# Start of a convolution, window-attention and linear-attention kernel: half of the first band's depthwise convolution on TensorE, and the order of the first loads

## The chip, the cores and the metric

One core of a Trainium2 chip runs the kernel. The metric is the time of one execution on the device in microseconds (us). Before the change it is 968.08 us, the median of three runs (965.33 to 969.31). The profiled execution has a span of 963.5 us.

## The reference, cut to what matters

The input x has 4 images of 128 channels and 64 x 64 pixels. Only the first part of layer 0 is touched by the change: a normalization over the channels, a depthwise 3x3 convolution with edge padding that is added to its input, and the products with the attention weights in windows of 16 x 16 pixels. What follows is named so that the reader can place it.

```python
def _layernorm2d(x, g, b):
    mean = x.mean(axis=1, keepdims=True)
    var = ((x - mean) ** 2).mean(axis=1, keepdims=True)
    return (x - mean) / jnp.sqrt(var + EPS) * g + b

def _cpe(x, w, b):                      # depthwise 3x3, one 3x3 filter for each channel
    xp = jnp.pad(x, ((0, 0), (0, 0), (r, r), (r, r)), mode='edge')
    y = jax.lax.conv_general_dilated(xp, w, (1, 1), 'VALID', feature_group_count=x.shape[1], ...)
    return y + b[None, :, None, None]

y = _layernorm2d(x, ln_g, ln_b)
y = y + _cpe(y, cpe_w, cpe_b)
xw = ...                                # y cut into windows of 16 x 16
q, k, v = ...                           # xw times Wq, Wk, Wv: 2 branches of 4 heads of 32
# attention of each pixel to its 5 x 5 neighbours in its window, weights Wo, added to x
# layer 1: LayerNorm, causal linear attention (W, b), added; LayerNorm, product W,
#          normalization over all tokens, a recurrence over the 4096 tokens (V), added
```

## The kernel before

An image is taken in 4 bands of 16 rows, so there are 16 bands; a band has 4 windows. Channels lie on the 128 partitions after the turning. TensorE does the products, VectorE the statistics and the taps of the convolution, ScalarE the evictions from PSUM and the exponentials, GpSimd small things and the division of the attention's output. Each compute engine executes its instructions in the order in which the program writes them (`in_order`). A generator that yields marks a gap, a place where the loop puts other work.

Normalization of a band: statistics of groups of rows, scaling one step later, turning and eviction one more step later.

```python
def norm_rows(n):
    ...
    for g in range(len(groups) + 2):
        if g < len(groups):
            found[g] = measured([...], 1e-6)              # VectorE, and rs on GpSimd
        if g - 1 in found:
            xn[g - 1] = normed(found.pop(g - 1), p2, "xf")    # VectorE, waits for rs
        if g - 2 in xn:
            rows = turned(xn.pop(g - 2), 0, j1 - j0)...       # TensorE, by ident
            evict(y[...], rows[...])                          # ScalarE, into ypad
        yield
    # GpSimd copies the edges of ypad
```

The convolution as nine taps: the first on ScalarE, eight on VectorE. In the first band each window has its own taps (256 columns), in the others half a band (512 columns).

```python
def taps(y2, y, c0, width, each):
    for tap in range(9):
        dy, dx = divmod(tap, 3)
        src = y[:, dy : dy + WS, c0 + dx : c0 + dx + width]
        if tap == 0:
            nc.scalar.activation(y2, src, AF.Identity, bias=cpe_b, scale=cpe_w[:, 0:1])
        else:
            nc.vector.scalar_tensor_tensor(y2, src, cpe_w[:, tap : tap + 1], y2, ALU.mult, ALU.add)
        if tap % each == 0:
            yield

def convolve_first(wj):
    ...
    run(taps(y2, ypads.pop(0) if wj == NB - 1 else ypads[0], wj * WS, WS, 8))
```

A window: `window_inputs` makes q, k and v (products, ScalarE evictions, two small transfers that put together the middle block of v), `logits` the scores and their exponentials `es`, `weighted` the sums of the weights and the weighted values, `scaled` the division.

```python
def weighted(w):
    # TensorE: dps <- ones, es
    den = p1.tile(...)
    nc.scalar.copy(den, dps)
    nc.sync.dma_start(dc, den[::HD, :])
    yield
    # TensorE: ops <- es, v
    o_sb = p1.tile(...)                     # p1: one buffer
    nc.scalar.copy(o_sb, ops)
    yield
    nc.vector.tensor_tensor(dc, dc, pad_c, ALU.add)
    nc.vector.reciprocal(rc, dc)
    ...
    nc.sync.dma_start(rd.rearrange("h (a e) -> (h a) e", e=16), rc)           # to DRAM
    nc.sync.dma_start(rden, rd.unsqueeze(1).to_broadcast([HEADS, HD, BR * WT]))   # and back, spread
    ...
def scaled(n, wj, w):
    nc.gpsimd.tensor_tensor(oTs[n][...], w["o"]..., w["rden"]..., ALU.mult)   # oT <- o_sb, rden
```

The start and the loop over the windows. `front` brings the norm and convolution of the bands ahead, `layer1` the rest of the band behind, a step in each gap.

```python
load(0)
load_head(1)
load(1)
run(norm_rows(0))
convolve_first(0)
windows = {0: {}}
run(window_inputs(windows[0], 0, 0))
ahead, behind = front(), iter(())

def between(i, gap):
    next(behind, None)
    if i < len(places) and (i % NB or gap in (0, 4, 5)) and (i or gap):
        next(ahead, None)

for i in range(len(places) + 2):
    ...
    logits(windows[i])
    ...
    between(i, 0)
    ...                                     # scaled of window i - 2
    sums = weighted(windows[i - 1]) if 1 <= i <= len(places) else iter(())
    for gap in (1, 2):
        next(sums, None)
        between(i, gap)
    run(sums)
    if i == 0:
        convolve_first(1)
    ...                                     # inputs = window_inputs of window i + 1
    for gap in (3, 4, 5):
        next(inputs, None)
        between(i, gap)
    run(inputs)
    if i == 0:
        convolve_first(2)
        convolve_first(3)
```

Ahead of this, eighteen loads of weights are issued from ScalarE's queue, and woT, ab and the middle tap's weight are prepared on VectorE.

Of the kernel before, what the change touches and what calls it, by code (L numbers as in the profile page):

```python
# [9 lines left out]
F32 = mybir.dt.float32  # L10
BF16 = mybir.dt.bfloat16
AF = mybir.ActivationFunctionType
ALU = mybir.AluOpType
AX = mybir.AxisListType
PSUM = bass.MemoryType.PSUM
ENGINES = [getattr(mybir.EngineType, e) for e in ("PE", "DVE", "Activation", "Pool")]

P = 128
B, H, W = 4, 64, 64
T = H * W  # L20
WS = 16
NB = H // WS
WT = WS * WS
BR, HEADS, HD = 2, 4, 32
# [3 lines left out]
NCH = BAND // P  # L28
BIG = 1.0e30
LAM = 0.5  # L30
# [16 lines left out]
def conv_attn_hybrid(ctx: ExitStack, tc: tile.TileContext, ins: dict, out: bass.AP):  # L47
    nc = tc.nc

    fast = ExitStack()  # L50
    const = fast.enter_context(tc.tile_pool(name="const", bufs=1))
# [6 lines left out]
    def loaded(name, shape, dt=F32, src=None, eng=None):  # L58
        t = const.tile(shape, dt, name=name)
        (eng or nc.sync).dma_start(t, ins[name] if src is None else src)  # L60
        return t

    ident = const.tile([P, P], F32, name="ident")
# [17 lines left out]
    mhalf = const.tile([P, NCH], F32, name="mhalf")  # L81
    nc.vector.memset(mhalf, -0.5)

    ln_g = loaded("ln_g", [P, 1], eng=nc.scalar)
    ln_b = loaded("ln_b", [P, 1], eng=nc.scalar)
    cpe_w = loaded("cpe_w", [P, 9], eng=nc.scalar)
    cpe_b = loaded("cpe_b", [P, 1], eng=nc.scalar)
# [3 lines left out]
    mask_k = loaded("mask_k", [P, P], BF16, eng=nc.scalar)  # L91
    mask_q = loaded("mask_q", [P, BR * WT], BF16, eng=nc.scalar)
    pad_c = loaded("pad_c", [P, 16], eng=nc.scalar)
    woT = loaded("woT", [P, BR, P], eng=nc.scalar)
    awT = loaded("awT", [P, 3 * P], eng=nc.scalar)
    ab = loaded("ab", [P, 3], eng=nc.scalar)
    abv = loaded("abv", [P, P], src=ins["abv"].partition_broadcast(P), eng=nc.scalar)
    fwT = loaded("fwT", [P, P], eng=nc.scalar)
    fvT = loaded("fvT", [P, P], eng=nc.scalar)
    gamma = loaded("gamma", [P, 1], eng=nc.scalar)  # L100
    beta = loaded("beta", [P, 1], eng=nc.scalar)


    nc.vector.tensor_scalar(cpe_w[:, 4:5], cpe_w[:, 4:5], 1.0, None, ALU.add)

    rect = math.sqrt(1.0 + LAM * LAM * (BR - 1))
    nc.vector.tensor_scalar(woT[:, 0], woT[:, 0], 1.0 / rect, None, ALU.mult)
    nc.vector.tensor_scalar(woT[:, 1], woT[:, 1], LAM / rect, None, ALU.mult)

    ab1 = const.tile([P, 2], F32, name="ab1")  # L110
    nc.vector.tensor_scalar(ab1, ab[:, :2], 1.0, None, ALU.add)

    dmax = const.tile([P, 16], F32, name="dmax")
    nc.vector.memset(dmax, 1.0)
# [5 lines left out]
    for i in range(2):  # L120
        t = const.tile([P, 4, P + 1], F32, name=f"v1_{i}")
# [3 lines left out]
    stats = const.tile([P, B * T // 512, 6], F32, name="stats")  # L125

    wx = const.tile([P, B, NH, SEG, HSEGS], F32, name="wx")

    main = ExitStack()
    p1 = main.enter_context(tc.tile_pool(name="p1", bufs=1))  # L130
    p2 = main.enter_context(tc.tile_pool(name="p2", bufs=2))
    p3 = main.enter_context(tc.tile_pool(name="p3", bufs=3))
    px = main.enter_context(tc.tile_pool(name="px", bufs=3))
    p6 = main.enter_context(tc.tile_pool(name="p6", bufs=6))
    ps = main.enter_context(tc.tile_pool(name="ps", bufs=8, space=PSUM))

    first = len(nc.cur_bb.bb.instructions)

# [16 lines left out]
    def bank():  # L155
        return ps.tile([P, 512], F32, tag="bank", name="bank")

    def run(g):
        for _ in g:
            pass  # L160

    bands = [(b, wi) for b in range(B) for wi in range(NB)]
    scale = HD ** -0.5

    def measured(pieces, eps):
# [27 lines left out]
        return tps  # L193


    xin = {}
    ypads = {}
    y2s = {}

    heads = {}  # L200

    def load_head(n):
        b, wi = bands[n]
        heads[n] = p1.tile([P, P], F32, tag="head", name="head")
        nc.sync.dma_start(heads[n], ins["xt"][b, wi, :, 0, :])

    def load(n):
        b, wi = bands[n]
        xin[n] = p3.tile([P, NCH, P], F32, tag="xin", name="xin")
        nc.sync.dma_start(xin[n], ins["xt"][b, wi])  # L210

    def padded(n):
        if n not in ypads:
# [3 lines left out]
    def norm_rows(n):  # L217

        b, wi = bands[n]
        y = padded(n)  # L220
        below = wi < NB - 1
        first, end = (0 if wi == 0 else 1), NCH + below

        def evict(dst, src):
            nc.scalar.activation(dst, src, AF.Identity, bias=ln_b, scale=ln_g)

        groups = [(0, 4), (4, 8), (8, 9)] if wi == 0 else [(1, 5), (5, end)]

        found, xn = {}, {}
        for g in range(len(groups) + 2):  # L230
            if g < len(groups):
                found[g] = measured(
                    [xin[n][:, j, :] if j < NCH else heads.pop(n + 1) for j in range(*groups[g])],
                    1e-6,
                )
            if g - 1 in found:
                xn[g - 1] = normed(found.pop(g - 1), p2, "xf")
            if g - 2 in xn:
                j0, j1 = groups[g - 2]
                rows = turned(xn.pop(g - 2), 0, j1 - j0)[:, : (j1 - j0) * P]  # L240
                rows = rows.rearrange("p (r w) -> p r w", w=W)
                k1 = min(2 * j1 + 1, WS + 2)
                evict(y[:, 2 * j0 + 1 : k1, 1 : W + 1], rows[:, : k1 - 2 * j0 - 1, :])
                if j1 > NCH:
                    evict(padded(n + 1)[:, 1:3, 1 : W + 1], rows[:, 2 * (NCH - j0) :, :])
            yield
        ks = slice(1, WS + 1 + below)
        nc.gpsimd.tensor_copy(y[:, ks, 0:1], y[:, ks, 1:2])
        nc.gpsimd.tensor_copy(y[:, ks, W + 1 :], y[:, ks, W : W + 1])

        if wi == 0:
            nc.gpsimd.tensor_copy(y[:, 0, :], y[:, 1, :])
        if below:
            nc.gpsimd.tensor_copy(padded(n + 1)[:, 0, :], y[:, WS, :])
        else:
            nc.gpsimd.tensor_copy(y[:, WS + 1, :], y[:, WS, :])
# [10 lines that stand above are left out]
            if tap % each == 0:  # L267
                yield

    def convolve_first(wj):  # L270

        half, k = divmod(wj, 2)
        if k == 0:
            y2s[0, half] = p2.tile([P, 2, WT], F32, tag="y2w", name="y2w")
        y2 = y2s[0, half][:, k, :].rearrange("p (r c) -> p r c", c=WS)
        run(taps(y2, ypads.pop(0) if wj == NB - 1 else ypads[0], wj * WS, WS, 8))

    def convolve(n, half):

# [341 lines left out]
    def front():  # L621


        for n in range(1, len(bands)):
            yield from norm_rows(n)
            if bands[n][1]:
                yield
            for half in range(2):
                yield from convolve(n, half)
                yield  # L630

    load(0)
    load_head(1)
    load(1)
    run(norm_rows(0))
    convolve_first(0)
    windows = {0: {}}
    run(window_inputs(windows[0], 0, 0))
    ahead, behind = front(), iter(())

    def between(i, gap):


        next(behind, None)
        if i < len(places) and (i % NB or gap in (0, 4, 5)) and (i or gap):
            next(ahead, None)

    for i in range(len(places) + 2):
        if i < len(places):
            n, wj = places[i]  # L650
            if wj == 0 and n + 1 < len(bands) and bands[n + 1][1] < NB - 1:
                load_head(n + 2)
            logits(windows[i])
        if 2 <= i:
            m, wjm = places[i - 2]
            if wjm == NB - 1:
                run(behind)
                behind = layer1(m, halves.pop(m - 1, (None, None)))
        between(i, 0)
        if 2 <= i:  # L660
            scaled(m, wjm, windows.pop(i - 2))
        if i < len(places) and wj == 1 and n + 2 < len(bands):
            load(n + 2)
# [3 lines that stand above are left out]
            between(i, gap)  # L667
        run(sums)
        if i == 0:
            convolve_first(1)  # L670
        inputs = iter(())
        if i + 1 < len(places):
            windows[i + 1] = {}
            inputs = window_inputs(windows[i + 1], *places[i + 1])
        for gap in (3, 4, 5):
            next(inputs, None)
            between(i, gap)
        run(inputs)
        if i == 0:
            convolve_first(2)  # L680
            convolve_first(3)
    run(behind)
    run(layer1_end(*halves.pop(len(bands) - 1)))
    in_order()
# [78 lines left out]
    for s in range(SEG):  # L763
        ys = ring.tile([P, B * SEGS], F32, tag="ys", name="ys")
        for g in range(NG):
            z = seeded(g, s)
            nc.tensor.matmul(z, fvT, last[g], start=False, stop=True, skip_group_check=True)
            y = ys[:, g * GC : (g + 1) * GC]
# [698 lines left out]
```

## Time and profile before

| | before |
|---|---|
| median of 3 runs | 968.08 us |
| span of the profiled execution | 963.5 us |
| TensorE busy | 872.7 us (91%) |
| VectorE busy | 756.2 us (78%) |
| ScalarE busy | 541.2 us (56%) |
| GpSimd busy | 259.7 us (27%) |

In the profile, PE is TensorE's products, PEld its loading of weights, DVE VectorE, ACT ScalarE, POOL GpSimd, SP SyncE; SPq and ACTq are the queues from which transfers are issued. An entry names the line of the kernel, the engine, the operation, and what it writes and reads. The chain of waits goes back from the last instruction, at each step to what released it; "issue" is time in which nothing shown was waited for. The time from 94 us to 889 us belongs to the dense middle of the kernel, the rest to the end with the recurrence.

### The profile page before, as it was taken

How to read it: one execution, taken by the hardware profiler on the slowest of the kernel's cores; microseconds unless marked ns; L12 is line 12 of the kernel's file. 1: busy time of each engine (PE TensorE's matmuls, PEld its weight loads, DVE VectorE, ACT ScalarE, POOL GpSimd, SP SyncE). 2: the span in 40 equal slices, each digit the busy share in tenths (PEclk: the TensorE clock that was granted, in tenths of full speed). 3: DMA queues.
4: the chain of work that ended last, by engine and by line, in shares of the span. 5: the costliest groups of instructions: out<-in, count | busy, mean ns of one | idle time of the engine just before them, and what ended most of it. 6: DMA issues, size and time to landing. Idle time of an engine off the chain costs nothing.

```text
span 963.5 us, 26493 instructions
## 1 busy us (share of the span) xinstructions
PE 872.7 (91%) x10472; PEld 649.9 (67%) x10472; DVE 756.2 (78%) x2468; ACT 541.2 (56%) x1001; POOL 259.7 (27%) x359
## 2 busy tenths in 40 slices
PE   2587999999999999999999999999999999978884
PEld 1365777778676777767777777676776778655442
DVE  4554897988787878888787978897988887577796
ACT  1454666565666656565656565666656565622553
POOL 2112222322314131323232221414131312131175
PEclk9788999999999999999999999999999999999798
DMA  3011112111212121121212111212112111110853
GB/s 117 12 38 39 57 58 57 53 54 56 57 49 69 36 78 37 47 57 59 57 55 57 53 52 54 64 47 70 37 54 58 45 36 58 42 39 22 352 205 146
DMA packets 52902, 63.47 MB, mean 66 GB/s; under 512 B 22944, under 2 KB 33824, under 8 KB 52256
## 3 DMA queue, kind: packets, MB, share of 16 engines
q1 hardware_dynamic: 49888, 56.38, 18.7%
q10 hardware_dynamic: 2880, 5.29, 1.4%
q8 instruction: 85, 1.39, 0.6%
q14 instruction: 49, 0.40, 0.1%
HBM read 35.44 MB, written 17.30 MB: 55 GB/s over the span
## 4 chain that ended last, share of the span: by engine, by line
PE 71%; DVE 11%; DMA 9%; ACT 4%; POOL 2%; issue 2%; SPq 1%; ACTq 0%; POOLq 0%; DVEq 0%
PE bank L297 10%; PE bank L342 6%; PE bank L425 6%; PE bank L192 6%; PE bank L372 6%; PE bank L360 5%; PE bank L310 5%; PE bank L454 5%; DMA rden<-rd 5%; PE bank L533 3%; PE bank L497 3%; PE bank L562 3%; PE bank L514 3%; PE bank L535 3%; DMA res<-resd 2%; PE bank L471 2%
## 5 line engine op out<-in xcount | busy, mean ns | idle before, releaser
L266 DVE SCALAR_TENSOR_TENSOR y<-ypad,cpe_w,y 128x512 f32<-128x512 f32 x240 | 189.8, 791 | 11.1 <-ACT y L264 7.6
L400 POOL TENSOR_TENSOR oT<-o_sb,rden 128x512 f32<-128x512 f32 x64 | 83.0, 1297 | 357.6 <-DMA rden<-rd 308.0
L351 ACT ACTIVATE es<-bank 128x512 f32<-128x512 f32 x256 | 132.2, 602 | 75.5 <-PE bank L342 75.5
L176 POOL TENSOR_TENSOR rs<-rs,mhalf 128x4 f32<-128x4 f32 (+2 forms) x100 | 107.2, 1072 | 8.3
L342 PEld LDWEIGHTS bank<-q,k 32*128 32x128 f32 x3072 | 97.8, 189 | 7.5 <-ACT k L305 6.2
L342 PE MATMUL bank<-q,k 32*128 32x96 f32 (+1 forms) x3072 | 96.3, 270 | 5.6 <-ACT k L305 5.6
L183 DVE TENSOR_SCALAR xn<-x,mv,rs 128x128 f32<-128x128 f32 x256 | 83.5, 387 | 21.6 <-POOL rs L176 21.6
L175 POOL TENSOR_SCALAR rs<-mv 128x4 f32<-128x4 f32 (+2 forms) x100 | 25.1, 251 | 278.0 <-DVE mv L173 190.0
L297 PE MATMUL bank<-y2w,wqT 128*128 128x256 f32 x256 | 68.7, 392 | 13.9 <-DVE y2w L266 13.2
L372 PEld LDWEIGHTS bank<-es,v_sb 128*32 128x32 f32 x3072 | 57.4, 111 | 29.9 <-issue 17.1
L380 ACT COPY o_sb<-bank 128x512 f32<-128x512 f32 x64 | 37.6, 587 | 60.5 <-POOL oT L400 47.5
L372 PE MATMUL bank<-es,v_sb 128*32 128x96 f32 (+1 forms) x3072 | 70.9, 241 | 0.0
L425 PE MATMUL bank<-woT,oT 128*128 128x128 f32 x512 | 65.3, 282 | 5.8 <-POOL oT L400 5.8
L454 PE MATMUL bank<-xl,awT 128*128 128x512 f32 x128 | 70.1, 631 | 0.3 <-ACT xl L449 0.3
L360 PE MATMUL bank<-es,ones 128*32 128x512 f32 x512 | 69.9, 619 | 0.0
L425 PEld LDWEIGHTS bank<-woT,oT 128*128 128x128 f32 x512 | 62.1, 195 | 9.6 <-POOL oT L400 6.8
L317 ACT COPY v_sb<-bank 128x512 f32<-128x512 f32 x64 | 37.6, 588 | 54.2 <-PE bank L310 53.5
L297 PE MATMUL bank<-y2w,wkT 128*128 128x256 f32 x256 | 67.6, 388 | 0.0
L310 PE MATMUL bank<-wvT,y2w 128*128 128x256 f32 x256 | 67.6, 387 | 0.0
L297 PEld LDWEIGHTS bank<-y2w,wqT 128*128 128x128 f32 x256 | 46.1, 196 | 25.9 <-issue 14.5
L305 ACT COPY q<-bank 128x512 f32<-128x512 f32 x64 | 37.8, 590 | 45.8 <-PE bank L297 45.5
L192 PE MATMUL bank<-ident,xf 128*128 128x128 f32 x128 | 31.2, 331 | 35.0 <-DVE xf L183 30.8
(120 smaller groups left out, 1747.3 us busy)
## 6 DMA issues: line engine op xcount, KB each, us to landing
rden<-rd SPq DMA_DIRECT2D x64, 256.0 KB
xin<-in_xt SPq DMA_DIRECT2D x16, 512.0 KB
v_sb<-v_sb SPq DMA_DIRECT2D x128, 64.0 KB
resd<-rs_o SPq DMA_DIRECT2D x32, 256.0 KB
out<-ot SPq DMA_DIRECT2D x32, 256.0 KB
res<-resd SPq DMA_DIRECT2D x2, 2048.0 KB
res<-resd ACTq DMA_DIRECT2D x2, 2048.0 KB
dc<-den SPq DMA_DIRECT2D x64, 8.0 KB
```

The source lines that it names most:

```text
L176: nc.gpsimd.tensor_tensor(rs[:, :n], rs[:, :n], mhalf[:, :n], ALU.pow)
L183: nc.vector.tensor_scalar(xn[:, j, :], piece, mv[:, j, 0:1], rs[:, j : j + 1], ALU.subtract, ALU.mult)
L192: nc.tensor.transpose(tps[:, j * P : (j + 1) * P], xn[:, j0 + j, :], ident)
L266: nc.vector.scalar_tensor_tensor(y2, src, cpe_w[:, tap : tap + 1], y2, ALU.mult, ALU.add)
L297: nc.tensor.matmul(pps[:, br * WT : (br + 1) * WT], wT[:, br * P : (br + 1) * P], y2, start=True, stop=True,)
L310: nc.tensor.matmul(vps[:, e * 256 : (e + 1) * 256], y2[:, e * P : (e + 1) * P], wvT, start=True, stop=True,)
L342: nc.tensor.matmul(sps[h][:, cols], w["k"][rows, k0 : k0 + P], w["q"][rows, cols], start=False, stop=(br, n) == pieces[-1],)
L351: nc.scalar.activation(es, sps[h], AF.Exp, scale=scale)
L360: nc.tensor.matmul(dps[rows], ones[:, :HD], w["es", h], start=True, stop=True)
L372: nc.tensor.matmul(ops[rows, cols], w["v"][:, n, c0 : c0 + HD], w["es", h][:, cols], start=(br, n) == pieces[0], stop=(br, n) == pieces[-1],)
L425: nc.tensor.matmul(yps[:, j * P : (j + 1) * P], oT[:, br, t], woT[:, br, :], start=br == 0, stop=br == BR - 1,)
L454: nc.tensor.matmul(zps, awT[:, m * P : (m + 1) * P], h.xl, start=True, stop=True)
```

## The change

Half of the first band's convolution, windows 2 and 3, is done on TensorE: a depthwise convolution is nine products with diagonal weights, added up in PSUM. The nine diagonals are written by ScalarE from the identity, into a part of wx that is not yet in use. The taps of windows 0 and 1 stay on VectorE and are both put ahead of window 0's products; window 2's nine products are put around those of window 0, window 3's after the logits of window 0. This is to keep TensorE from standing while VectorE convolves. The loads of x come first, the first band's in two pieces; weights that are needed later are loaded from SyncE's queue behind x, and prepared after the taps, so that the first scaling of x doesn't stand behind them. The next band's norm begins one gap earlier, and four empty steps after the second band put the rest of the sequence where it was.

```diff
+    load(0, 2)
+    load_head(1)
     ln_g = loaded("ln_g", [P, 1], eng=nc.scalar)
     ...                                            # cpe_w, cpe_b, wqT, wkT, wvT, masks: as before
     pad_c = loaded("pad_c", [P, 16], eng=nc.scalar)
-    woT = loaded("woT", [P, BR, P], eng=nc.scalar)
-    awT = loaded("awT", [P, 3 * P], eng=nc.scalar)
-    ...                                            # ab, abv, fwT, fvT, gamma, beta
-    nc.vector.tensor_scalar(cpe_w[:, 4:5], cpe_w[:, 4:5], 1.0, None, ALU.add)
-    ...                                            # woT and ab prepared
+    load(1)
+    woT = loaded("woT", [P, BR, P])
+    awT = loaded("awT", [P, 3 * P])
+    ...                                            # ab, abv, fwT, fvT, gamma, beta
+    def prepare():
+        ...                                        # woT and ab prepared

+    diag = wx[:, B - 1].rearrange("p n s k -> p (n s k)")[:, : 9 * P]
+    diag = diag.rearrange("p (t c) -> p t c", c=P)
+
+    def multiply_first(wj):
+        half, k = divmod(wj, 2)
+        if k == 0:
+            y2s[0, half] = p2.tile([P, 2, WT], F32, tag="y2w", name="y2w")
+        y = ypads.pop(0) if wj == NB - 1 else ypads[0]
+        cps = bank()[:, :WT]
+        for tap in range(9):
+            dy, dx = divmod(tap, 3)
+            src = y[:, dy : dy + WS, wj * WS + dx : wj * WS + dx + WS]
+            nc.tensor.matmul(cps, diag[:, tap, :], src, start=tap == 0, stop=tap == 8)
+            if tap == 3:
+                yield
+        nc.scalar.activation(y2s[0, half][:, k, :], cps, AF.Identity, bias=cpe_b)

     # front()
+            if n == 1:
+                for _ in range(4):
+                    yield

-    load(0)
-    load_head(1)
-    load(1)
+    nc.vector.tensor_scalar(cpe_w[:, 4:5], cpe_w[:, 4:5], 1.0, None, ALU.add)
+    for tap in range(9):
+        nc.scalar.activation(diag[:, tap, :], ident, AF.Copy, scale=cpe_w[:, tap : tap + 1])
     run(norm_rows(0))
+    load_head(2)
     convolve_first(0)
+    convolve_first(1)
+    prepare()
+    third, fourth = multiply_first(2), multiply_first(3)
+    next(third)
     windows = {0: {}}
     run(window_inputs(windows[0], 0, 0))
+    run(third)

     # between(i, gap)
-        if i < len(places) and (i % NB or gap in (0, 4, 5)) and (i or gap):
+        if i < len(places) and (i == 0 or i % NB or gap in (0, 4, 5)):

     # the loop over the windows
-        if i == 0:
-            convolve_first(1)
+        if i == 0:
+            run(fourth)
     ...
-        if i == 0:
-            convolve_first(2)
-            convolve_first(3)
```

More of the change, by code (lines that the diff above doesn't have):

```diff
@@ L82, in conv_attn_hybrid, with load_head, load @@
     nc.vector.memset(mhalf, -0.5)
+    main = ExitStack()
+    p1 = main.enter_context(tc.tile_pool(name="p1", bufs=1))
+    p2 = main.enter_context(tc.tile_pool(name="p2", bufs=2))
+    p3 = main.enter_context(tc.tile_pool(name="p3", bufs=3))
+    px = main.enter_context(tc.tile_pool(name="px", bufs=3))
+    p6 = main.enter_context(tc.tile_pool(name="p6", bufs=6))
+    ps = main.enter_context(tc.tile_pool(name="ps", bufs=8, space=PSUM))
+    bands = [(b, wi) for b in range(B) for wi in range(NB)]
+    xin = {}
+    heads = {}
+    def load_head(n):
+        b, wi = bands[n]
+        heads[n] = p1.tile([P, P], F32, tag="head", name="head")
+        nc.sync.dma_start(heads[n], ins["xt"][b, wi, :, 0, :])
+    def load(n, pieces=1):
+        b, wi = bands[n]
+        xin[n] = p3.tile([P, NCH, P], F32, tag="xin", name="xin")
+        for k in range(pieces):
+            js = slice(k * NCH // pieces, (k + 1) * NCH // pieces)
+            nc.sync.dma_start(xin[n][:, js, :], ins["xt"][b, wi, :, js, :])
+    load(0, 2)
+    load_head(1)
     ln_g = loaded("ln_g", [P, 1], eng=nc.scalar)
@@ L93, in conv_attn_hybrid @@
     pad_c = loaded("pad_c", [P, 16], eng=nc.scalar)
-    woT = loaded("woT", [P, BR, P], eng=nc.scalar)
-    awT = loaded("awT", [P, 3 * P], eng=nc.scalar)
[L96 to L101, printed above, removed]
-    nc.vector.tensor_scalar(cpe_w[:, 4:5], cpe_w[:, 4:5], 1.0, None, ALU.add)
-    rect = math.sqrt(1.0 + LAM * LAM * (BR - 1))
-    nc.vector.tensor_scalar(woT[:, 0], woT[:, 0], 1.0 / rect, None, ALU.mult)
-    nc.vector.tensor_scalar(woT[:, 1], woT[:, 1], LAM / rect, None, ALU.mult)
-    ab1 = const.tile([P, 2], F32, name="ab1")
-    nc.vector.tensor_scalar(ab1, ab[:, :2], 1.0, None, ALU.add)
+    load(1)
+    woT = loaded("woT", [P, BR, P])
+    awT = loaded("awT", [P, 3 * P])
+    ab = loaded("ab", [P, 3])
+    abv = loaded("abv", [P, P], src=ins["abv"].partition_broadcast(P))
+    fwT = loaded("fwT", [P, P])
+    fvT = loaded("fvT", [P, P])
+    gamma = loaded("gamma", [P, 1])
+    beta = loaded("beta", [P, 1])
+    ab1 = const.tile([P, 2], F32, name="ab1")
+    def prepare():
+        rect = math.sqrt(1.0 + LAM * LAM * (BR - 1))
+        nc.vector.tensor_scalar(woT[:, 0], woT[:, 0], 1.0 / rect, None, ALU.mult)
+        nc.vector.tensor_scalar(woT[:, 1], woT[:, 1], LAM / rect, None, ALU.mult)
+        nc.vector.tensor_scalar(ab1, ab[:, :2], 1.0, None, ALU.add)
     dmax = const.tile([P, 16], F32, name="dmax")
@@ L127, in conv_attn_hybrid @@
     wx = const.tile([P, B, NH, SEG, HSEGS], F32, name="wx")
[L129 to L135, printed above, removed]
     first = len(nc.cur_bb.bb.instructions)
@@ L160, in run @@
             pass
-    bands = [(b, wi) for b in range(B) for wi in range(NB)]
     scale = HD ** -0.5
@@ L193, in turned @@
         return tps
-    xin = {}
     ypads = {}
     y2s = {}
[L200 to L210, printed above, removed]
     def padded(n):
@@ L275, in convolve_first @@
         y2 = y2s[0, half][:, k, :].rearrange("p (r c) -> p r c", c=WS)
-        run(taps(y2, ypads.pop(0) if wj == NB - 1 else ypads[0], wj * WS, WS, 8))
+        run(taps(y2, ypads[0], wj * WS, WS, 8))
     def convolve(n, half):
@@ L650, in conv_attn_hybrid @@
             n, wj = places[i]
-            if wj == 0 and n + 1 < len(bands) and bands[n + 1][1] < NB - 1:
+            if i and wj == 0 and n + 1 < len(bands) and bands[n + 1][1] < NB - 1:
                 load_head(n + 2)
```

## The prediction

> **What bounds the kernel now.** I read three views: the busy time by stretches of the span, to see which stage has room; the chain of waits of the first 100 us, to see what sets the end of that stage; and the timeline of that stage, for durations and for the order on each engine. The stretches come first. Columns: stretch and its length in us, then busy us (and instructions) of each engine, granted TensorE clock, DMA share, GB/s.
>
> ```profile
> 0.00:20.00 20.00, 2.90 (x9) 1.64 (x9) 9.30 (x45) 4.09 (x6) 5.04 (x17) 1.00 0.47 140
> 20.00:40.00 20.00, 11.56 (x74) 9.01 (x75) 8.52 (x31) 5.38 (x10) 2.42 (x4) 0.77 0.03 8
> 40.00:60.00 20.00, 13.49 (x215) 9.51 (x218) 12.25 (x28) 10.04 (x20) 1.69 (x4) 0.80 0.11 31
> 60.00:94.00 34.00, 25.07 (x410) 18.03 (x400) 17.68 (x49) 19.03 (x37) 6.45 (x8) 0.90 0.14 40
> 94.00:144.00 50.00, 48.44 (x635) 36.85 (x633) 42.43 (x140) 29.33 (x54) 13.61 (x19) 1.00 0.18 56
> ```
>
> From 94 us on TensorE is busy 97% of the time, and the later bands look the same (49.7 of 51, 50.7 of 52). Nothing of the diff is executed there. Before 94 us TensorE is busy 53.0 of 94 us: this start of 94 us is all that the change can shorten. What is saved before 94 us is kept, for the stages behind it only start earlier. The chain of waits of the start (start us, length us, what):
>
> ```profile
> 7.96 3.48 DMA woT<-in_woT
> ...
> 16.73 0.61 ACT y2w L264
> 17.37 0.49 DVE y2w L266
> ...
> 21.55 3.78 PE bank L297 x8
> ...
> 31.45 0.49 DVE y2w L266
> ...
> 35.72 3.75 PE bank L297 x8
> ...
> 42.31 0.49 DVE y2w L266
> ...
> 50.88 1.15 PE bank L192 x4
> ```
>
> The reader sees that TensorE stands three times for VectorE's eight taps of a window (17.37 to 21.55, 31.45 to 35.72, and both last windows 42.31 to 50.4), and that the first scaling of x stood for woT, a weight that it doesn't need.
>
> The same chain, later, in the part between 60 and 94 us:
>
> ```profile
> 72.58 0.05 ACT o_sb L380
> ...
> 74.66 0.51 SPq L319
> ...
> 75.22 1.23 SPq L320
> ...
> 76.55 5.17 DMA rden<-rd
> ...
> 81.85 1.27 POOL oT L400
> ```
>
> This is a ring: o_sb has one buffer, so its eviction waits for oT of the window before; behind it ScalarE evicts q, k, v; SyncE then issues the two v_sb transfers and only behind them rden; oT waits for rden; the next o_sb is at 83.15. One turn is 83.15 - 72.58 = 10.57 us. The change doesn't touch this ring, so it limits how much of an early gain gets through.
>
> [...] the four records of the q product take 2.08 us at 21.55, after 6.3 us idle, and 1.13 us at 60.61, in the middle of work (timeline):
>
> ```profile
> 21.55 2.08 PE L297 MATMUL bank<-y2w,wqT 128*128 128x256 f32 x4 [6.28 <-DVE y2w L266]
> 60.61 1.13 PE L297 MATMUL bank<-y2w,wqT 128*128 128x256 f32 x4
> ```
>
> [...] the scaling at 11.73 starts only when the scaling of woT, which is ahead of it on VectorE and waited for its transfer, is done, although its own rs has been there since 9.5.
>
> **The change, part by part.**
> (1) The weights from woT on leave ScalarE's queue and go behind x on SyncE's; their scaling on VectorE moves behind the taps of windows 0 and 1. On VectorE rs is ready at 9.5 (GpSimd's 8.48 + 1.03), the scaling starts then and not at 11.73: 2.2 us earlier. But ScalarE now has work ahead of its first eviction: it ends its ten DMA issues at 7.9, loads its table (1.28 us), to 9.2, and writes nine diagonals of 128x128. The 128x64 form of the eviction takes 0.40 us and the 128x128 form 0.47 us, each overlapping its neighbour by about 0.1 us, so about 0.37 us apiece, 3.3 us for nine: to 12.5. The first eviction then starts at 12.5 and not at 13.47. The later ones no longer wait 0.65 us for TensorE: 12.5 + 0.78 + 1.43 ends at 14.7, not 16.33. Gain 1.6 us; tap 0 of window 0 starts at 15.1, its eight VectorE taps run 15.75 to 19.9, the q product of window 0 starts at 19.95 instead of 21.55.
> (2) Windows 2 and 3 go to TensorE: two times nine products of 128x256. A product of this shape took 3.75 / 4 = 0.94 us cold with its start, 0.855 us in a run of cold ones (1.71 for two), and 0.43 warm (0.86 for two). Cold the nine are 7.7 us, warm 3.85 us. Four taps of window 2 stand at 15.1 to 18.5, while TensorE would only wait: free. Its other five stand between the v product and the logits of window 0: on the path. The products of window 0 run 19.95 to about 24.7 (q and k cold, 3.4 us; v half warm, 1.3 us), the five taps take 2.15 to 4.3 us, I choose 2.6: logits at 27.3, where they were at 26.97. So the 1.6 us are spent here.
> (3) Window 3's nine taps stand ahead of window 1's q product, warm: 3.85 us. VectorE has done window 1 long before (19.9 to 24.1), and the statistics of band 1 too. TensorE: logits of window 0 to 29.1, four turns of band 1's norm 0.66, taps to 33.6, q, the other turns, k and v 0.86 + 0.66 + 1.72 to 36.9. Logits of window 1 start at 36.9 instead of 41.08: 4.2 us gained.
> (4) Behind them nothing waits for VectorE any more. Logits 1.9 us to 38.8, the four exponentials 2.06 us to 41.0, den of window 0 at 41.0 instead of 45.40. VectorE formerly reached dc of window 0 only at 51.42, behind sixteen taps; now its transfer (1.85 us, row of window 1) and at most one tap stand before it: about 44. Its rd is issued at 44.6 instead of 51.96, 7.4 us earlier; rden follows 2.2 us later and takes 4.7 to 5.2, oT 1.3: o_sb of window 1 at 53.0 instead of 61.21.
> (5) Now the ring of 10.57 us per turn begins one window earlier, because o_sb of window 1 waits for oT, where before it hardly did. And two ScalarE instructions of band 1's convolution, which used to lie in ScalarE's idle time at 67.06 and 68.05, come into the turn: the copy y2w (start to start 0.5 us) and tap 0 (0.75 us), 1.25 us. From o_sb to the issue of rden is 76.55 - 72.58 = 3.97 us: rden of window 1 at 53.0 + 3.97 + 1.25 = 58.2 instead of 66.47: 8.3 us gained. The second copy of y2w costs the next turn 0.5 us. Left: 7.8 us. The other turns are as before, so oT of window 3 ends at 93.6 - 7.8 = 85.8, and from there the program is the same.
> Sum: 968.08 - 7.8 = 960.3; I say 960.
>
> **The rivals.**
> (a) The convolution on TensorE stays cold or its strided rows of 16 read slowly. For it: TensorE idles about 1.4 us at 18.5, and at 35.72 it took over 5 us to get warm (a product pair still took 1.7 us at 39.47). Against: from 19.95 it is no longer idle. It would add 1.7 us in (2) and up to 3.85 us in (3), leaving 2 to 4 us: 964 to 966.
> (b) The ring does not bind as I have it, and the whole advance of the logits of window 2 (57.0 to about 43.5, 13.5 us) gets through: 955. Against it is that rden of window 1 stands behind v_sb of window 3 on SyncE, which stands behind o_sb.
> (c) The start is hidden anyway: TensorE's dense stage takes the loss back. Against it: at 93.64 the output product waits for oT, and then TensorE is 97% busy. Time 967 to 968.
> (d) Nine more ScalarE instructions and the weights queued on SyncE make the start later (woT late, or x in two pieces landing later). The scaling of woT would have to be later than 24 us to matter for VectorE's statistics; all loads had landed by about 13 us before. Time 970.
>
> **Range and chances.** What is sure: sixteen VectorE taps leave the path, and with them the waits of TensorE of 6.5 to 7 us ahead of 35.72 and 50.88; the ring lets only part of that through. Clock phases carry some 3 us of doubt downwards, (b) 5 upwards; the runs before spread over 4 us. So 960, 8 in 10 within 954 to 966. Faster by over 2% would need 19.4 us, that is oT of window 3 at 74, under the ring's three turns: 0.03. Slower by over 2%: 0.01. Within 2%: 0.96.
>
> **What would show each step right or wrong.** First q product at 19.9 (1); logits of window 0 near 27.3 and five taps of about 0.45 to 0.85 us ahead of them (2); logits of window 1 near 36.9 (3); first rd near 44.6 (4); o_sb evictions near 53, 65, 76 and 86 with the wait on oT (5); the first output product near 86 instead of 93.64, and the bands behind it with the same spacing, about 51 us. The prediction is wrong if the first output product moves by much more or less than 8 us, or if the spacing of the later bands changes.

## The result, and the profile after

The changed kernel takes 953.37 us (median of 4 runs, 951.26 to 954.82) against 968.69 us (4 runs, 965.33 to 969.47); the ratio is 0.9847, interval 0.9816 to 0.9877. A second measurement of the same kernel, beside the kernel before, gave 0.9849 (0.9812 to 0.9886). The prediction was 960, range 954 to 966: the direction and the stage were right, but the gain is about 15 us where 7.8 were expected, just outside the range.

The busy time by stretches, profile after (columns as before), cut where the start now ends:

```profile
0.00:20.00 20.00, 8.25 (x24) 5.58 (x25) 11.90 (x48) 7.49 (x17) 5.03 (x17) 1.00 0.47 141
20.00:40.00 20.00, 19.41 (x230) 15.56 (x230) 9.31 (x36) 12.48 (x24) 3.02 (x7) 1.00 0.07 18
40.00:60.00 20.00, 14.89 (x245) 10.63 (x244) 12.85 (x25) 10.01 (x20) 2.52 (x2) 0.91 0.15 43
60.00:79.00 19.00, 14.82 (x234) 9.74 (x235) 5.91 (x28) 10.75 (x22) 4.93 (x6) 0.82 0.17 48
79.00:129.00 50.00, 48.42 (x631) 36.90 (x634) 42.30 (x140) 29.46 (x54) 13.60 (x19) 1.00 0.18 56
```

The dense middle begins at 79 us instead of 94 and looks as before: 48.42 us of TensorE in its first 50 us, against 48.44. Between 20 and 40 us TensorE is now busy 97% of the time (before: 11.56 of 20). From 40 us on it waits again. The first output product is at 78.78 us instead of 93.64, 14.86 us earlier, and that of the next band keeps the distance (129.25 against 144.09). Behind the first output product the profiles are 872.0 us long after and 869.9 before, so that the whole spans differ by 12.7 us only. The profiled execution of before was its fastest run, 965.33 us.

The chain of waits of the start, after:

```profile
8.80 2.43 ACT wx L664 x8
...
13.61 0.61 ACT y2w L271
14.25 0.50 DVE y2w L273
...
22.41 0.14 DVE woT L137
...
25.24 0.36 DVE xf L203
...
25.73 1.00 PE bank L212 x4
26.74 3.98 PE bank L291 x18
30.72 0.86 PE bank L322 x4
...
42.00 4.83 DMA rden<-rd
46.97 1.27 POOL oT L425
48.26 0.05 ACT o_sb L405
...
51.55 0.51 SPq L344
...
52.11 0.59 SPq L345
...
52.80 4.71 DMA rden<-rd
57.65 1.27 POOL oT L425
58.95 0.05 ACT o_sb L405
...
69.00 0.05 ACT o_sb L405
...
78.78 2.06 PE bank L450 x16
```

It leads over the diagonals, the taps of windows 0 and 1 on VectorE, the scaling of woT, the statistics and scaling of band 1, and its turning (L212), then over window 3's nine products (L291 x18, two records each) and the ring. The wait for woT's transfer is gone. TensorE's waits of 6 to 7 us for taps are gone too; what is left of them is 1.02 us ahead of the first q product, for window 0's taps, and 0.58 us ahead of 25.73, for band 1's scaling, which stands behind the sixteen taps of windows 0 and 1. The ring is there as predicted, entered at 48.26 us (before: 61.21, without a wait for oT). From o_sb to o_sb its turns are 10.69, 10.05 and 9.76 us; in the kernel before they are 11.37, 10.57 and 10.47.

| start of, us | before | predicted | after | again |
|---|---|---|---|---|
| first q product | 21.55 | 19.95 | 18.43 | 17.80 |
| logits of window 0 | 26.97 | 27.3 | 23.44 | 24.89 |
| logits of window 1 | 41.08 | 36.9 | 33.68 | 34.12 |
| rd of window 0 | 51.96 | 44.6 | 40.38 | 40.82 |
| o_sb of window 1 | 61.21 | 53.0 | 48.26 | 49.53 |
| first output product | 93.64 | 85.8 | 78.78 | 80.41 |

"Again" is the same kernel in the second measurement.

### The profile page after: what moved, and what is told of

Same layout as the page of the kernel before. It is cut to its first block, busy times and chain, and to the rows that moved or that the text cites. A ratio compares the mean times of both kernels' runs of the same rounds, so it can differ in the third digit from the quotient of the medians.

```text
span 950.8 us, 26560 instructions
## 1 busy us (share of the span) xinstructions
PE 878.3 (92%) x10508; PEld 654.2 (69%) x10508; DVE 745.0 (78%) x2452; ACT 542.6 (57%) x1010; POOL 260.4 (27%) x359
## 3 DMA queue, kind: packets, MB, share of 16 engines
q10 hardware_dynamic: 1728, 4.77, 1.3%
## 4 chain that ended last, share of the span: by engine, by line
PE 71%; DMA 10%; DVE 9%; ACT 4%; POOL 3%; issue 2%; SPq 1%; ACTq 0%; POOLq 0%; DVEq 0%
PE bank L322 9%; PE bank L367 6%; PE bank L450 6%; PE bank L212 6%; PE bank L385 6%; PE bank L397 6%; DMA rden<-rd 5%; PE bank L479 5%; PE bank L335 5%; PE bank L558 3%; PE bank L587 3%; PE bank L522 3%; PE bank L539 3%; PE bank L560 3%; DMA res<-resd 2%; PE bank L496 2%
## 5 line engine op out<-in xcount | busy, mean ns | idle before, releaser
L203 DVE TENSOR_SCALAR xn<-x,mv,rs 128x128 f32<-128x128 f32 x256 | 80.3, 374 | 21.5 <-POOL rs L196 21.5
L385 PE MATMUL bank<-es,ones 128*32 128x512 f32 x512 | 72.5, 640 | 0.0
L450 PE MATMUL bank<-woT,oT 128*128 128x128 f32 x512 | 65.9, 283 | 5.2 <-POOL oT L425 5.2
L450 PEld LDWEIGHTS bank<-woT,oT 128*128 128x128 f32 x512 | 62.7, 197 | 9.0 <-POOL oT L425 6.2
L322 PE MATMUL bank<-y2w,wqT 128*128 128x256 f32 x256 | 66.3, 382 | 1.0 <-DVE y2w L273 1.0
L191 DVE BATCH_NORM_STATS2 st<-x 128x6 f32<-128x128 f32 x256 | 55.5, 279 | 1.1
L212 PE MATMUL bank<-ident,xf 128*128 128x128 f32 x128 | 30.6, 328 | 25.4 <-DVE xf L203 21.1
```

The source lines that it names most:

```text
L212: nc.tensor.transpose(tps[:, j * P : (j + 1) * P], xn[:, j0 + j, :], ident)
L322: nc.tensor.matmul(pps[:, br * WT : (br + 1) * WT], wT[:, br * P : (br + 1) * P], y2, start=True, stop=True,)
L385: nc.tensor.matmul(dps[rows], ones[:, :HD], w["es", h], start=True, stop=True)
L450: nc.tensor.matmul(yps[:, j * P : (j + 1) * P], oT[:, br, t], woT[:, br, :], start=br == 0, stop=br == BR - 1,)
```

## The experiments

Each ratio is to the kernel before on the same chip. "Output product" is the start of the first one, L450's first instruction, in that run's profile.

**Taps behind.** My first theory, the clock theory, was that the four taps in the gap had made q, k and v quick (2.69 us).

```diff
-    next(third)
```

> The changed kernel with all nine taps of window 2 behind window 0's products, none ahead of them. Clock theory (the four taps in the gap warmed TensorE, so that q, k and v ran at full rate): the q product starts at 18.4 us as before, q, k and v take about 4.7 us instead of 2.7 and the nine taps 3.9 instead of 2.4, logits of window 0 near 27 us instead of 23.4, first output product near 82 us instead of 78.8, time 956 to 957.5. Work theory (the gap only took in four taps of work, TensorE would be warm anyway): logits of window 0 near 25.1, first output product near 80.5, time 955.

Ratio 0.9879 (0.9859 to 0.9899), 959.70 us. q, k and v took 4.1 us, logits of window 0 started at 25.97, output product 81.84. From the q product (17.79) to those logits it is 8.2 us, between the two theories (8.6 and 6.7) and nearer to the clock theory. The ratio is that of the clock theory, whose 956 to 957.5 of 968.69 us is 0.987 to 0.988.

**Warm only.** The same, with four products in the gap whose result isn't read.

```diff
-    next(third)
+    idle_bank = bank()[:, :WT]
+    for tap in range(4):
+        dy, dx = divmod(tap, 3)
+        src = ypads[0][:, dy : dy + WS, 2 * WS + dx : 3 * WS + dx]
+        nc.tensor.matmul(idle_bank, diag[:, tap, :], src, start=tap == 0, stop=tap == 3)
```

> As the kernel with the taps behind, but four products of the same shape whose result nobody reads stand in the gap ahead of window 0's products (extra work, no useful work in the gap). Clock theory: q, k and v in 2.7 us, logits of window 0 near 25.1 us, time near 955, some 2 us below the kernel with the taps behind. Work theory: the same time as the kernel with the taps behind.

Ratio 0.9893 (0.9864 to 0.9921), 959.91 us, output product 81.73. q, k and v were slow with the products ahead of them, 4.36 us. The clock theory as I had it falls: four products in this gap did not make q, k and v quick here.

**The changed kernel once more**, unaltered.

> The changed kernel once more, unaltered, beside the others on one chip. If the full-rate q, k and v of its first trace come from the four taps ahead of them, they are at full rate here too (2.7 us together) and logits of window 0 start near 23.4 us less the shift of the loads. If that was chance of the clock's phase, they may be cold here (4 to 5 us together) and logits of window 0 start near 25 us. Ratio to before 0.983 to 0.988 either way.

Ratio 0.9849 (0.9812 to 0.9886), 957.68 us. Here q, k and v were slow. The timelines of the two executions of the same program, first profile and then this one:

```profile
18.43 1.13 PE L322 MATMUL bank<-y2w,wqT 128*128 128x256 f32 x4 [1.02 <-DVE y2w L273]
```

```profile
13.00 3.78 PE L291 MATMUL bank<-ypad,wx 128*128 128x256 f32 x8 [1.86 <-POOL ypad L259]
17.80 2.08 PE L322 MATMUL bank<-y2w,wqT 128*128 128x256 f32 x4 [1.02 <-DVE y2w L273]
```

The same four records take 1.13 us in one and 2.08 us in the other, after the same 1.02 us of idle time. From the q product to the taps behind v it is 2.69 us and 4.77 us. Of the eight profiles with window 2's four taps in the gap and nothing else there, four were quick (2.7 us) and four slow (4.6 to 5.0). What decides between the two, no run shows. Clock, cold and warm were my names for it; the granted clock doesn't follow it: in the kernel before it is 1.00 over the slow products of window 0 (21.55 to 25.30 us) and 0.50 over those of window 1 (35.70 to 41.00), and in the changed kernel 1.00 over the quick ones (18.43 to 21.00).

**Kept warm.** Nine small unread products fill the gaps from the first turns to the q product.

```diff
+    filler = bank()[:, :P]
+    for _ in range(4):
+        nc.tensor.matmul(filler, ident, ident, start=True, stop=True)
     next(third)
+    filler2 = bank()[:, :P]
+    for _ in range(5):
+        nc.tensor.matmul(filler2, ident, ident, start=True, stop=True)
```

> The changed kernel with nine small products of the identity whose result nobody reads, four ahead of window 2's first four taps and five behind them, so that TensorE has almost no idle time from the first turn to the first q product. Clock theory: the taps themselves or at least q, k and v run at full rate in every execution, logits of window 0 at 22.5 to 23.5 us, and the time is 1 to 2 us under the changed kernel on the same chip. Rival (clock at the start does not matter, the ring takes it back): the same time within 1 us, or slower where the five stand in the way of the q product.

q, k and v took 2.70 us, logits of window 0 started at 22.84, the output product was at 79.00, 1.4 us before that of the kernel once more. Of these, 1.0 us is there at rd of window 0 (39.78 against 40.82); the rest arises behind it, where the first rden took 5.24 us against 5.65. The ratio is 0.9837 (0.9809 to 0.9866), the median 957.88 us: no difference to 0.9849 that can be measured. That the unread products made it quick is not shown by one profile, as half of the others were quick without them.

What a quick start is worth can be read from the profiles that have their q product at 17.8 us and the changed kernel's order up to there. The logits of window 0 start at 22.81 and 22.84 in the two quick ones, at 24.72 to 25.14 in the four slow ones: 2 us. The logits of window 1 start at 33.05 and 33.09 against 33.96 to 34.37: 1 us, since in the quick ones TensorE then waits for band 1's scaling (0.59 us in both). So slow or quick first products move this start by about 1 us from execution to execution, and are a small part of the missed 7 us.

**Loads only.** The new loads and the late preparation, the convolution as before.

```diff
-    for tap in range(9):
-        nc.scalar.activation(diag[:, tap, :], ident, AF.Copy, scale=cpe_w[:, tap : tap + 1])
 ...   # no multiply_first; convolve_first(1), (2), (3) at their old places, old gaps
```

> The kernel before with the new order and queues of the loads and the later preparation of woT and ab, convolution all on ScalarE and VectorE, as before. If the loads are worth what they move at the first q product: that product near 17.5 us instead of 21.55, first output product near 89.6 us instead of 93.6, time 964 to 965. Rival: the ring of o_sb and rden, or a VectorE that is busy anyway, takes it back: first output product above 92 us, time 967 to 968.

The first q product is at 17.59, as expected, the output product at 88.16. The time is 969.68 us, ratio 0.9972 (0.9956 to 0.9989): 2.7 us. The 3 to 4 us that were expected lie within this interval, the 5.5 us by which the output product lies ahead of that of before don't. Behind the output product this profile is 879.6 us long, before's 869.9. Some 6 us of the difference are that before's profile is of a run of 965.33 us, where its median beside this kernel is 971.62; what the rest is, no run shows. At its ring two issues of v_sb took 1.70 and 1.42 us (at 58.81 and 70.48).

**Convolution only.** The convolution on TensorE with the loads of before.

```diff
 ...   # all weights from ScalarE's queue, woT and ab prepared at once, load(0) in one piece
+    load(0)
+    load_head(1)
+    load(1)
     for tap in range(9):
         nc.scalar.activation(diag[:, tap, :], ident, AF.Copy, scale=cpe_w[:, tap : tap + 1])
```

> The change without its part on the loads: all weights from ScalarE's queue ahead of everything, woT and ab prepared ahead of the first scaling, x in one piece behind; the convolution on TensorE as changed. The nine diagonals now stand behind eighteen issues (to 12.1) and the table load, so they end near 16.2 us and the first eviction starts there. First q product near 24 us instead of 18.4 (before 21.55), first output product near 84 us, time about 6 us above the changed kernel, ratio to before 0.99. Rival: the order of the loads hardly matters here: within 2 us of the changed kernel.

Ratio 0.9919 (0.9888 to 0.995), 966.71 us; first q product 24.19, output product 85.20. This is 9.0 us above the changed kernel once more, where 6 were expected. The diagonals and the first eviction stand in the timeline in the expected order, 0.7 us later than expected:

```profile
14.25 2.74 ACT L662 ACTIVATE wx<-ident,cpe_w 128x128 f32<-128x128 f32 x9
16.89 2.06 ACT L228 ACTIVATE ypad<-bank,ln_b,ln_g 128x512 f32<-128x512 f32 x4
```

Alone the convolution is worth 0.8%, the loads alone 0.3%, both 1.5%; with these intervals that is not shown to be more than the sum. At the first q product they are more together: the loads alone bring it 4.0 us forward, the convolution alone puts it 2.6 us back, both bring it 3.1 and 3.75 us forward. The nine diagonals go through ScalarE, and start at 14.25 us behind the eighteen issues, at 8.49 behind ten. At the first output product the two parts add up: 5.5 and 8.4 us alone, 14.9 and 13.2 together.

**Two buffers** for o_sb and rden, in the changed kernel: does the ring bind?

```diff
-        o_sb = p1.tile([P, BR * WT], F32, tag="o_sb", name="o_sb")
+        o_sb = p2.tile([P, BR * WT], F32, tag="o_sb", name="o_sb")
-        rden = p1.tile([P, BR * WT], F32, tag="rden", name="rden")
+        rden = p2.tile([P, BR * WT], F32, tag="rden", name="rden")
```

> The changed kernel with two buffers instead of one for o_sb and for rden. Ring theory (o_sb waits for oT of the window before, and SyncE's rden stands behind transfers that wait for o_sb): the three turns of about 10 us shrink to TensorE's own 6.5 us, first output product near 68 to 70 us instead of 78.8, time 942 to 945. Rival (the latency of dc, rd and rden sets the pace anyway, or the dense stage takes it back): time 951 to 953.

Ratio 0.9711 (0.969 to 0.9732), 943.51 us: it beats both kernels. The time is the expected one, but not by the expected way. The output product came at 74.98, not at 68 to 70. The rest lies in the later bands: behind the output product this profile is 867.9 us long, against 872.0 and 872.9 in the two profiles of the changed kernel. There, too, o_sb had waited for oT. From the lists of waits of the kernel before and of the changed kernel (who waited for what: us in total, times, longest):

```profile
ACT o_sb L380 <- POOL oT L400: 47.5, 32, 3.8
ACT o_sb L405 <- POOL oT L425: 51.9, 32, 4.0
```

With two buffers one wait of 0.3 us is left. What stops the start now is in its chain of waits:

```profile
44.98 3.11 DMA dc<-den
48.11 1.26 DVE dc L408
...
55.25 0.76 DVE y L273
...
56.03 0.05 ACT y2w L309
...
57.67 2.89 PE bank L367 x48
```

dc of window 1, then the eight taps of band 1 that stand behind it on VectorE, then their copy, and q and k of window 3 behind that on ScalarE.

**o_sb alone** and **rden alone**: one line of the last diff each.

> The changed kernel with two buffers for o_sb alone, rden keeps one. Ring theory (the link that binds is o_sb waiting for oT of the window before, with q, k, v and then SyncE's rden behind it): the second o_sb eviction no longer waits, and nearly all of the gain of two buffers is there: first output product near 75 us, ratio to before 0.970 to 0.975. Rival (rden's own buffer binds as well, rden 4.9 + oT 1.3 us per window): ratio near that of the changed kernel, 0.983 to 0.986.

> The changed kernel with two buffers for rden alone, o_sb keeps one. Ring theory: no effect, first output product at 79 to 81 us, ratio to before 0.983 to 0.987. Rival (rden's buffer binds): much of the gain of two buffers, ratio below 0.979.

With o_sb doubled the ratio is 0.9701 (0.9666 to 0.9735), 945.73 us, output product 74.62. With rden doubled it is 0.9797 (0.976 to 0.9835), 956.01 us, output product 80.70, where the kernel once more had 80.41; the ratio is a little below the expected band, but its interval reaches into it, and the place of the output product shows no effect. The link that binds is o_sb's single buffer.

**The kernel before with two buffers.**

> The kernel before with two buffers for o_sb and rden. If the ring bounds the start of the kernel before too: first output product near 85 us instead of 93.6 and the time 8 us or more below before, ratio 0.99 or less; the change on top of two buffers (changed kernel with two buffers: 943.5 us against 971.6) is then worth about what the logits of window 2 moved, 17 us. If the ring bounds only the changed kernel: time within 2 us of before.

Ratio 0.9881 (0.9853 to 0.991), 961.58 us, output product at 90.01 and not 85. The ring bound the kernel before too, mostly in later bands: of the 11.9 us 3.6 are there at the output product, and behind it o_sb's waits for oT, 32 before, are two of 1.0 us together. The change on top of two buffers is 0.9711 against 0.9881, 1.7% or some 17 us; that this is more than the 1.5% without is within the intervals. At the output product the change is worth 15.0 us with two buffers (90.01 to 74.98), 14.9 and 13.2 with one: at most 2 us held back by the single buffer.

**Taps early**, on top of two buffers.

```diff
-        yield from taps(y2, y, half * 2 * WS, 2 * WS, 1 + half)
+        yield from taps(y2, y, half * 2 * WS, 2 * WS, 2 if n == 1 else 1 + half)
...
-                for _ in range(4):
+                for _ in range(8):
```

> Both buffers doubled, and the second band's taps of its first half two to a gap instead of one, so that its second half's taps stand ahead of dc of window 1 and its copy no longer holds q of window 3 back (in the kernel with two buffers eight VectorE taps and the copy stood in the chain between 49.7 and 56.6 us). If that is what binds now: first output product 2 to 4 us earlier than the 75.0 of two buffers, ratio to before 0.968 or less. Rival (the dense stage or dc's own wait takes it): within 1 us of two buffers, 0.970 to 0.972.

Ratio 0.9682 (0.9643 to 0.972), 943.98 us; output product 74.70. That is no gain that can be measured: 0.3 us at the output product, and the interval contains the 0.9711 of two buffers. ScalarE's copy of y2w at 51.92 still waits for taps of VectorE, after 4.01 us of idle time; and from the issue of the fourth dc, at 61.16, to that of its rd it is 5.72 us, where with two buffers it is 3.02 (from 63.15); why it is longer, no run shows.

**Old gaps.** The changed kernel with the old condition in `between` and without the four empty steps.

```diff
-        if i < len(places) and (i == 0 or i % NB or gap in (0, 4, 5)):
+        if i < len(places) and (i % NB or gap in (0, 4, 5)) and (i or gap):
-            if n == 1:
-                for _ in range(4):
-                    yield
```

> The changed kernel without its new gaps: the next band's norm one step later as before, no four empty steps. If the copy y2w and tap 0 of the second band inside the ring cost what the prediction said (1.25 and 0.5 us): first output product 1 to 2 us earlier than the changed kernel's 78.8 to 80.4, time 1 to 2 us less. Rival: the new gaps are needed, the norm of band 1 comes too late for what follows: later, ratio to before above 0.987.

Ratio 0.9819 (0.9776 to 0.9863), 955.61 us; output product 77.20. The first turns of the ring are 9.78 and 9.90 us instead of 10.69 and 10.05. From o_sb to the issue of rden, where the added ScalarE instructions stand, it is 3.33 and 3.35 us instead of 4.54 and 3.85: they cost 1.2 and 0.5 us, 1.7 in all, as predicted. Part of it is hidden in the turns because rden and oT took 0.3 us longer in each of them here. The time lies in the expected direction, but the intervals overlap, so that a gain in time is not shown.

| kernel | q, k, v, us | output product, us | ratio |
|---|---|---|---|
| before | | 93.64 | 1 |
| changed / once more | 2.69 / 4.77 | 78.78 / 80.41 | 0.9847 / 0.9849 |
| taps behind | 4.10 | 81.84 | 0.9879 |
| warm only | 4.36 | 81.73 | 0.9893 |
| kept warm | 2.70 | 79.00 | 0.9837 |
| loads only | | 88.16 | 0.9972 |
| convolution only | 2.69 | 85.20 | 0.9919 |
| two buffers | 5.02 | 74.98 | 0.9711 |
| o_sb alone | 2.69 | 74.62 | 0.9701 |
| rden alone | 4.96 | 80.70 | 0.9797 |
| before, two buffers | | 90.01 | 0.9881 |
| two buffers, taps early | 4.61 | 74.70 | 0.9682 |
| old gaps | 2.70 | 77.20 | 0.9819 |

## Why the prediction missed, step by step

What bounds, where the gain arises and that it is kept behind 94 us: right. The order of events of (1) to (5) is the one in the trace. What failed is the size of the advance in step (5), in two terms. At the ring's entry, o_sb of window 1, the sum of (1) to (4) had 8.2 us; 12.95 and 11.7 were measured. And from there on I took the ring's turns over from the kernel before, 32.8 us with what the change adds, where 30.5 and 30.9 were measured. Together that is 7.8 us predicted at the first output product and 14.9 measured.

**(1) Start, 1.6 us predicted; 3.1 and 3.75 measured.** ScalarE ended its ten issues and began its table load at 7.20, and at 6.55 in the second profile, not at 7.9: the pause between its fifth and sixth issue ended at 4.38 and 3.83, before at 5.18. What ends it, no run shows. Nine diagonals took 2.74 us, 0.30 apiece and not 0.37. The eviction began at 11.14 and 10.50, not 12.5. At the q product that is 1.5 us in the first profile, 2.15 in the second.

**(2) First products, chosen slow** as in the kernel before (2.08 us for the four records at 21.55). The 4.75 us that I had calculated for q, k and v were 4.77 in the second profile, and 2.69 in the first, where all was quick. This is 0 to 2.1 us at the logits of window 0; that idle time ahead of them decides it was not shown: it was 1.02 us in both. I had put the doubt about this at 3 us, my estimate, on the side of a smaller gain; in the first profile it fell on the other side.

**(3) Near in its size, wrong about a wait:** from the logits of window 0 to those of window 1 9.6 us predicted, 10.2 and 9.2 measured. I had the statistics of band 1 done long before; in the quick first profile TensorE waits 0.58 us for the scaling behind them, so that part of the luck in (2) is lost again. Rival (a) is out: from the start of window 3's nine products on strided rows to that of the q product behind them it is 3.98 us in both profiles, 0.44 apiece, where the quick ones of the same shape in the kernel before took 0.86 us for two.

**(4) dc to rd:** from the logits of window 1 to rd of window 0 7.7 us predicted, 6.7 measured in both profiles. 0.44 us of it lie ahead of den, which came 3.66 us behind the logits and not 4.1; most of the rest is a tap of VectorE that I had put in front of dc and that was already done.

**(5) The ring, mis-sized.** From o_sb of window 1 to the output product I had 32.8 us; it took 30.5 and 30.9. The turn of 10.57 us that I took over from the kernel before contained an issue of v_sb that lasted 1.23 us; the next one there, at 85.79, lasted 1.50. In the changed kernel the same issue lasts 0.59 to 0.60. The one of the third turn, before and after:

```profile
85.79 1.50 SPq L320 DMA_DIRECT2D v_sb<-v_sb  x1
```

```profile
71.64 0.60 SPq L345 DMA_DIRECT2D v_sb<-v_sb  x1
```

My sum has the 1.23 us in two turns and the 1.50 in one, so 0.64 + 0.64 + 0.90 = 2.2 us in it are not there in the changed kernel: nearly all of the 2.3 us of this step. The ScalarE instructions that I added for cost what I had (old gaps). So the turn that I treated as a constant is 9.9 us without the long issue.

The first profile's miss adds up: 1.5 (start) + 2.1 (first products) + 0.3 (window 2's five taps, 2.3 us instead of 2.6) - 0.6 (3) + 1.0 (4) + 0.5 (rd to o_sb) + 2.3 (ring) = 7.1 us, and 85.8 - 78.8 = 7.0. In the second profile it is 2.15 (start) + 0 (first products) + 0.3 + 0.4 (3) + 1.0 (4) - 0.3 (rd to o_sb, where the first rden took 5.65 us and not 4.83) + 1.9 (ring), that is 5.4 us within rounding.

**The rivals.** The number of rival (b), 955, was nearest, its mechanism only in part right. The logits of window 2 came 17.0 us earlier (57.00 to 39.99; I had 13.5), and 12.95 of them were left at o_sb of window 1, which waited 4.0 us for oT: the ring does bind, and doubling o_sb alone takes another 1.5% off. But at the output product it held back 2 us (3 in the second profile), where I had nearly 6, because its turns were shorter than before. (c) and (d) are out.

What stays open: why some issues of v_sb last 1.2 to 1.7 us. In the first 90 us they stand in all three profiles of kernels with the old convolution (three, two and one) and in none of the nine with part of it on TensorE whose SyncE queue was read, so it does not look like chance, but no run isolates what makes them.

## What to carry to other kernels

Where a chain of waits has many terms, an error of a tenth in each adds up if all were chosen on the careful side: choose middle values, and widen the range on both sides. A turn of a ring read from the trace is one sample: its neighbours, 11.37 and 10.47 us here, looked alike, and only its parts showed it (an issue of 1.23 us, 0.59 at 58.28 and 65.77), so compare each part with its fellows before multiplying the turn. And a single buffer that shows as a repeated wait is worth a trial of a second one: here that brought almost as much as the whole change.

## What the runs showed of the hardware

The same program, with the same 1.02 us of idle time ahead, ran the four records of its first q product in 1.13 us in one execution and in 2.08 us in another, and four products in a gap did not settle it: of eight profiles four were quick (2.69 to 2.70 us for q, k and v) and four slow (4.61 to 5.02). With products over nearly the whole gap the one profile taken was quick (2.70 us), which is too few to tell. VectorE's dc, 128x16, took 0.17 us at 39.89 and 0.91 us at 47.35 in the changed kernel, the second time beside GpSimd's oT (46.97 to 48.23). Issues of the same small transfer on SyncE, v_sb, lasted 0.46 to 0.69 us as a rule; of 128, six in the kernel before and four in the changed one took longer than 0.7 us, the longest 1.80.
